# Linear attention and gated FFN on one core: the last residual added whole, and the last pair's end in float32 halves

## The chip, the cores and the metric

The kernel runs on one core of one Trainium2 chip. The metric is the device time of one execution in microseconds (us). A core has a matrix engine (TensorE, PE in the profile; its weight loads are PEld), three element-wise engines (VectorE or DVE, ScalarE or ACT, GpSimd or POOL) and a queue engine (SyncE, SP). Each engine works through its own queue in order; they wait for each other through semaphores. TensorE writes to PSUM, which has eight banks of 128 x 512 float32; SBUF holds everything else.

## The reference

```python
x = L0_attn_inputs_embeds                         # (16, 256, 128)
x = _layernorm(x + _L0_attn_ref(x, Wqkv, bqkv, Wproj, bproj))
x = _layernorm(x + _L0_ffn_ref(x, w_gate, w_up, w_down))

def _L0_attn_ref(x, ...):                         # 12 layers, 16 heads of 8
    for i in range(12):
        q, k, v = split(x @ Wqkv[i].T + bqkv[i])
        att = q @ k.T / sqrt(8)                   # per head, no softmax
        x = (att @ v) @ Wproj[i].T + bproj[i] + x
    return x

def _L0_ffn_ref(x, w_gate, w_up, w_down):         # int weights times 1/127
    h = silu(x @ w_gate.T / 127) * (x @ w_up.T / 127)     # 384 hidden
    return h @ w_down.T / 127
```

The change is in the last line of the main part: the FFN, the residual sum and the second layer norm.

## The kernel before

The attention has no softmax, so the kernel carries a 128 x 130 matrix per batch through the 12 layers instead of the 256 tokens; tokens come back only at the end. This part fills about the first 240 us.

The 16 batches form eight **pairs** (`NP` = 8) of 512 tokens. `ffn(p, prio)` (L578) issues one pair's end. Tokens stand as four chunks of 128. In order:

- **Residual and first norm.** Transposes of the carried matrix (L644), small bf16 pieces of its offset column (L657), then the tokens' products into one bank (L663, L665). `norm` (L590) takes statistics on VectorE (L602, two chunks an instruction), variance (L603), and on GpSimd the power -1/2 (L609); the scaling into `x1` is either one VectorE op (L616) or four ScalarE ops (L621).
- **Transposes of x1** into a bank (`tr_x`, L671). The bank is split into a high part `xh` in float32r, a rounded float32 that TensorE takes in one pass (a copy, L204 on ScalarE), and a low part `xl` (VectorE, L674). Two float32r passes, one of `xh` and one of `xl`, make up one product.
- **Three hidden blocks** of 128 (`NH` = 3). Each has a gate and an up product (L681 and L682, two passes of 512 columns each), SiLU on ScalarE (L684), the multiply on VectorE (L685) into `sg`, a split of `sg` into `hh` (the helper `copy`, L204 on ScalarE or L206 on VectorE) and `hl` (the helper `sub`, L209 on GpSimd or VectorE), and the down product of both (L693, L694), summed over the blocks in one bank.
- **The residual.** The sum after the FFN needs xh + xl. `xh` is added on VectorE (L696) when the bank is read, times 1/127. `xl` comes in by one more TensorE pass in block 0: `id127r`, 127 times the identity, times `xl` (L692).
- **Second norm.** Transposes back to token order (`tr_o`, L702), statistics, variance, negated mean (L605), power and product on GpSimd (L609, L611), four scalings on ScalarE (L625), and a store (L708) from SyncE. For the last pair the transposes go to two banks, VectorE scales the first half (L623) and ScalarE the second, and ScalarE issues that half's store.

`xt`, `qgv`, `kv`, `yhl`, `thl` in the profile are buffers of the attention part that the FFN uses again: `x1` is `kv`, `sg0` is `xt`, `sg1` is in `qgv`, `xh` is `yhl`, `xl` is `thl`.

**What sets the order.** Nothing is issued when it is called. `plan.op(costs, emit, reads, writes, prio)` records an operation with a cost per engine that could do it; `Plan.run` then goes through the ready operations in a modelled time, takes among those that can start earliest the one of lowest `prio` (less a small share of the work behind it), picks its engine and its bank, and emits it. The order of each engine's queue, the choice between ScalarE, VectorE and GpSimd, and the banks all follow from these costs. `prio` rises by `FSTEP` = 0.15 from pair to pair, so eight pairs are interleaved, the earlier ones ahead:

```python
for p in range(NP):
    ffn(p, L + FOFF + FSTEP * p)
```

Of the kernel before, what the change touches and what calls it, by code (L numbers as in the profile page):

```python
# [9 lines left out]
F32 = mybir.dt.float32  # L10
F32R = mybir.dt.float32r
# [3 lines left out]
ALU = mybir.AluOpType  # L15
# [3 lines left out]
L = 12  # L19
B = 16  # L20
T = 256
C = 128
H = 16
D = C // H
NH = 3
PB = 2
NP = B // PB
W = C + 2
QSCALE = 1.0 / 127.0
# [5 lines left out]
N = PB * T  # L35
K = N // 128
# [12 lines left out]
FOFF = -1  # L49
FSTEP = 0.15  # L50
LSTEP = 0.05
WLEAD = 0.6
TAILW = 0.0001
SPARE = 500


# [16 lines left out]
PE, ACT, DVE, POOL, SP = "pe", "act", "dve", "pool", "sp"  # L73
# [19 lines left out]
class Plan:  # L93
# [3 lines left out]
    def op(self, costs, emit, reads=(), writes=(), prio=0.0):  # L97

        o = Op(len(self.ops), costs, emit, prio)
        for v in reads:  # L100
            o.deps.update(v.writers)
        for v in writes:
            o.deps.update(v.writers, v.readers)
            v.writers, v.readers = [o], []
        for v in reads:
            if v not in writes:
                v.readers.append(o)
        o.vals = list(dict.fromkeys([*reads, *writes]))
        for v in o.vals:
            if v.kind:  # L110
                v.left += 1
                v.ops.append(o)
        for d in o.deps:
            d.users.append(o)
        self.ops.append(o)
# [50 lines left out]
def mm32(n=C):  # L166
    return max(220, 4 * n / 2.4 + 8)


def mmr(n):  # L170
    return max(111, 0.447 * n + 5)


def act(n, sbuf=False, pointers=0):
    return (94 if sbuf else 51) + 93 * pointers + n / 1.2


def dve(n, fast=False):
    return 69 + n / (1.92 if fast else 0.96)


def pool(n):
    return 147 + 2.1 * n
# [7 lines left out]
def linear_attention_ffn_kernel(ctx: ExitStack, tc: tile.TileContext, x, xt, wall, wq0, bias, wg, wu, wd, out):  # L191
    nc = tc.nc
# [3 lines left out]
    new = lambda name, shape, dt=F32: sb.tile([128, *shape], dt, name=name)  # L196
# [3 lines left out]
    bank = lambda v: banks[v.slot]  # L200

    def copy(e, dst, src):
        if e == ACT:
            nc.scalar.copy(dst, src)  # L204
        else:
            (nc.vector if e == DVE else nc.gpsimd).tensor_copy(dst, src)  # L206

    def sub(e, dst, a, b):
        (nc.vector if e == DVE else nc.gpsimd).tensor_tensor(dst, a, b, ALU.subtract)  # L209
# [17 lines left out]
    ident = new("ident", [128])  # L227
# [5 lines left out]
    center, centerr = new("center", [128]), new("centerr", [128], F32R)  # L233
    nc.gpsimd.tensor_scalar(center, ident, 1.0, -1.0 / C, ALU.mult, ALU.add)
    nc.vector.tensor_copy(centerr, center)

    id127, id127r = new("id127", [128]), new("id127r", [128], F32R)
    nc.gpsimd.tensor_scalar(id127, ident, 1.0 / QSCALE, 0.0, ALU.mult, ALU.add)
    nc.vector.tensor_copy(id127r, id127)
    mhalf = new("mhalf", [K])  # L240
    nc.gpsimd.memset(mhalf, -0.5)

# [335 lines left out]
    def ffn(p, prio):  # L578
# [8 lines left out]
        def op(costs, emit, reads, writes):  # L587
            plan.op(costs, emit, reads, writes, prio)

        def norm(src, centred, other=None):  # L590


            xs, rows = t("x1"), lambda: bank(src)
            cut = lambda a, k: a[:, k * C : (k + 1) * C]
            row = lambda k: cut(bank(other if other and k >= K // 2 else src), k)

            def stats(e):

                for k in range(0, K, 2):
                    b = bank(other if other and k else src)  # L600
                    both = b[:, k * C : (k + 2) * C].rearrange("p (k c) -> p c k", c=C)
                    nc.vector.bn_stats(t("st")[:, k : k + 2, :].rearrange("p k s -> p (k s)"), both)  # L602
                nc.vector.tensor_scalar(t("ve"), t("st")[:, :, 2], 1.0 / C, EPS, ALU.mult, ALU.add)  # L603
                if not centred:
                    nc.vector.tensor_scalar(t("nm"), t("st")[:, :, 1], -1.0, None, ALU.mult)  # L605
            op({DVE: K // 2 * (dve(2 * C) + 40) + 75 * (2 - centred)}, stats, [src, *([other] if other else [])], [v["st"]])

            def rstd(e):
                nc.gpsimd.tensor_tensor(t("rs"), t("ve"), mhalf, ALU.pow)  # L609
                if not centred:  # L610
                    nc.gpsimd.tensor_tensor(t("nb"), t("nm"), t("rs"), ALU.mult)  # L611
            op({POOL: 1060 + 220 * (not centred)}, rstd, [v["st"]], [v["rs"]])

            def scale(e, ks=range(K)):
                if centred and e == DVE:
                    nc.vector.tensor_tensor(chunks(xs), chunks(rows()), t("rs").unsqueeze(2).to_broadcast([128, K, C]), ALU.mult)  # L616
                    return
                for k in ks:
                    d, r, rs = cut(xs, k), row(k), t("rs")[:, k : k + 1]
                    if centred:  # L620
                        nc.scalar.activation(d, r, AF.Copy, scale=rs)  # L621
                    elif e == DVE:
                        nc.vector.tensor_scalar(d, r, t("st")[:, k, 1:2], rs, ALU.subtract, ALU.mult)  # L623
                    else:
                        nc.scalar.activation(d, r, AF.Identity, bias=t("nb")[:, k : k + 1], scale=rs)  # L625
            if centred:
                costs = {DVE: dve(N), ACT: K * act(C, False, 1)}
            else:
                costs = {ACT: K * act(C, False, 2)}
            if not other:  # L630
                op(costs, scale, [src, v["rs"], v["st"]], [v["x1"]])
                return [v["x1"]]

            ends = [Val(), Val()]
            op({DVE: 2 * 319}, lambda e: scale(e, range(2)), [src, v["rs"], v["st"], v["x1"]], [ends[0]])
            op({ACT: 2 * act(C, False, 2)}, lambda e: scale(e, range(2, K)), [other, v["rs"], v["st"], v["x1"]], [ends[1]])
            return ends


        ptt, pc, pr, px, pd, po = (Val("bank") for _ in range(6))  # L640

        def tr_t(e):
            for b in range(PB):
# [28 lines left out]
        op({PE: K * 109}, tr_x, [v["x1"]], [px])  # L672
        op({ACT: act(N), DVE: dve(N)}, lambda e: copy(e, t("xh"), bank(px)), [px], [v["xh"]])
        op({DVE: dve(N)}, lambda e: nc.vector.tensor_tensor(t("xl"), bank(px), t("xh").bitcast(F32), ALU.subtract), [px, v["xh"]], [v["xl"]])  # L674
        for n in range(NH):
            sg, hh, hlo = f"sg{n % 2}", f"hh{n % NB}", f"hl{n % NB}"
            pgate, pup = Val("bank"), Val("bank")
            for key, o in (("g", pgate), ("u", pup)):
                def mm_x(e, key=key, o=o, n=n):
                    ws = fw[key][:, n * C : (n + 1) * C]  # L680
                    nc.tensor.matmul(bank(o), ws, t("xh"), start=True, stop=False)  # L681
                    nc.tensor.matmul(bank(o), ws, t("xl"), start=False, stop=True)  # L682
                op({PE: 2 * mmr(N)}, mm_x, [v["xh"], v["xl"], vfw[key]], [o])
            op({ACT: act(N)}, lambda e, sg=sg, o=pgate: nc.scalar.activation(t(sg), bank(o), AF.Silu, scale=QSCALE), [pgate], [v[sg]])  # L684
            op({DVE: dve(N)}, lambda e, sg=sg, o=pup: nc.vector.scalar_tensor_tensor(t(sg), bank(o), QSCALE, t(sg), ALU.mult, ALU.mult), [pup], [v[sg]])  # L685
            op({ACT: act(N, True), DVE: dve(N, True)}, lambda e, sg=sg, hh=hh: copy(e, t(hh), t(sg)), [v[sg]], [v[hh]])
            op({POOL: pool(N), DVE: dve(N)}, lambda e, sg=sg, hh=hh, hlo=hlo: sub(e, t(hlo), t(sg), t(hh).bitcast(F32)), [v[sg], v[hh]], [v[hlo]])

            def mm_d(e, n=n, hh=hh, hlo=hlo):
                ws = fw["d"][:, n * C : (n + 1) * C]  # L690
                if n == 0:
                    nc.tensor.matmul(bank(pd), id127r, t("xl"), start=True, stop=False)  # L692
                nc.tensor.matmul(bank(pd), ws, t(hh), start=False, stop=False)  # L693
                nc.tensor.matmul(bank(pd), ws, t(hlo), start=False, stop=(n == NH - 1))  # L694
            op({PE: (2 + (n == 0)) * mmr(N)}, mm_d, [v[hh], v[hlo], v["xl"], vfw["d"]], [pd])
        op({DVE: dve(N)}, lambda e: nc.vector.scalar_tensor_tensor(t("sg0"), bank(pd), QSCALE, t("xh").bitcast(F32), ALU.mult, ALU.add), [pd, v["xh"]], [v["sg0"]])  # L696

        po2 = Val("bank") if p == NP - 1 else None

        def tr_o(e):  # L700
            for k in range(K):
                nc.tensor.transpose(bank(po2 if po2 and k >= K // 2 else po)[:, k * C : (k + 1) * C], t("sg0")[:, k * 128 : (k + 1) * 128], ident)  # L702
        op({PE: K * 109}, tr_o, [v["sg0"]], [po, *([po2] if po2 else [])])
        ends = norm(po, False, po2)
        m = N // len(ends)
        for i, end in enumerate(ends):
# [20 lines left out]
            center_tokens(l, l + 2)  # L727
    prep_ffn(L - 2)
    for p in range(NP):
        ffn(p, L + FOFF + FSTEP * p)  # L730
    plan.run()


# [29 lines left out]
```

## Time and profile before

| | |
|---|---|
| runs shown | 309.02 us median of 3 (308.63 to 309.62) |
| profiled execution | 309.26 us, its span 307.2 us |
| granted TensorE clock, mean | 0.989 |
| busy share of the span: PE, DVE, ACT, POOL | 97%, 74%, 72%, 44% |
| chain that ended last, by engine | PE 88%, DVE 7%, ACT 3% |

The span runs from the first to the last instruction; the execution's time has some 2 us more around it. The groups of instructions that belong to the change, from 240 us on:

| group | count | mean of one |
|---|---|---|
| L692 PE, 127 times the identity, 512 columns | 8 | 448 ns |
| L693, L694 PE, down product, 512 columns | 24, 24 | 402, 404 ns |
| L204 ACT, cast to `hh` | 21 | about 645 ns |
| L206 DVE, cast to `hh` | 3 | 1449 ns (one), 622 ns (two) |
| L209 POOL, `hl` | 14 | 1.30 us |
| L209 DVE, `hl` | 10 | 809 ns (nine), 683 ns (one) |
| L621 ACT, scaling of the first norm, 128 columns | 24 | 399 ns |
| L616 DVE, the same, 512 columns at once | 2 | 682 ns |
| L696 DVE, last sum, 512 columns | 8 | 681 ns |
| L702 PE, transposes back | 32 | 293 ns |

The mean of one is how long its record lasts. Records overlap in an engine's pipeline (a pass of 0.39 us may start 0.23 us after the one ahead), so a sum over a queue is made with the distance between starts.

### The profile page before, as it was taken

The page shows a single profiled execution, that of the slowest core. Times are in us where ns is not written, and L with a number is a line of the kernel's source. Part 1 is how long each engine was busy: PE and PEld are TensorE (multiplying, and loading weights), DVE is VectorE, ACT ScalarE, POOL GpSimd, SP SyncE. Part 2 cuts the span into 40 slices and gives each one's busy share as a digit, 9 for nine tenths or more (in the row PEclk, how much of TensorE's full clock was granted, in tenths as well). Part 3 has the DMA queues.
Part 4 walks back from the last instruction along what each step waited for, and adds up shares of the span by engine and source line. Part 5 has one row for each costly group of instructions (what it writes and reads, how often), then busy time and mean ns, then how long its engine had stood idle before and what let it go on. Part 6 is the DMA issues. An engine that isn't in the chain of part 4 may idle for free.

```text
span 307.2 us, 12904 instructions
## 1 busy us (share of the span) xinstructions
PE 297.3 (97%) x5384; PEld 272.3 (89%) x5384; DVE 227.2 (74%) x680; ACT 221.3 (72%) x571; POOL 136.4 (44%) x234
## 2 busy tenths in 40 slices
PE   8999999999999999999999999999999999999971
PEld 8989999999999999999999999999999988888840
DVE  3797887777677676776767877787554699899993
ACT  2547877867768677777677666776986768968964
POOL 6246353334541345314453144521442456568582
PEclk9999999999999999999999999999999999999995
DMA  7534213122031120311202112130000000000214
GB/s 211 149 99 128 71 39 89 35 55 71 9 82 38 42 84 2 90 37 43 82 4 53 38 28 55 30 81 2 4 2 3 2 1 2 0 0 22 83 34 137
DMA packets 22489, 15.65 MB, mean 51 GB/s; under 512 B 1952, under 2 KB 19872, under 8 KB 22432
## 3 DMA queue, kind: packets, MB, share of 16 engines
q1 hardware_dynamic: 21872, 14.62, 17.5%
q8 instruction: 42, 0.69, 0.9%
q10 hardware_dynamic: 560, 0.22, 0.3%
q14 instruction: 15, 0.12, 0.1%
HBM read 8.02 MB, written 2.10 MB: 33 GB/s over the span
## 4 chain that ended last, share of the span: by engine, by line
PE 88%; DVE 7%; ACT 3%; issue 1%; POOLq 0%; POOL 0%
PE bank L460 14%; PE bank L439 8%; PE bank L522 8%; PE bank L441 7%; PE bank L440 7%; PE bank L447 5%; PE bank L504 5%; PE bank L541 4%; PE bank L539 4%; PE bank L540 4%; PE bank L448 3%; PE bank L449 3%; PE bank L341 3%; PE bank L665 2%; PE bank L681 2%; PE bank L682 2%
## 5 line engine op out<-in xcount | busy, mean ns | idle before, releaser
L209 POOL TENSOR_TENSOR thl<-tst,thl 128x260 fp32r<-128x260 f32 x88 | 64.5, 764 | 122.9 <-ACT thl L204 122.9
L204 ACT COPY qgv<-bank 128x256 f32<-128x256 f32 x171 | 60.8, 376 | 20.5 <-PE bank L449 13.5
L204 ACT COPY kv<-bank 128x512 f32<-128x512 f32 (+1 forms) x93 | 53.3, 575 | 18.6 <-PE bank L441 13.4
L439 PE MATMUL bank<-whl,thl 128*128 128x256 f32 x176 | 51.8, 294 | 0.0
L441 PE MATMUL bank<-whl,thl 128*128 128x256 f32 x176 | 49.6, 282 | 0.0
L440 PE MATMUL bank<-whl,thl 128*128 128x256 f32 x176 | 49.4, 281 | 0.0
L460 PE MATMUL bank<-kv,g 128*128 128x128 f32 x352 | 46.0, 275 | 0.0
L546 DVE TENSOR_TENSOR tst<-bank,tst 128x260 f32<-128x260 f32 x96 | 36.9, 425 | 11.9 <-PE bank L541 9.1
L204 ACT CAST thl<-tst 128x260 fp32r<-128x260 f32 x88 | 33.0, 408 | 14.6 <-DVE tst L546 14.5
L460 PEld LDWEIGHTS bank<-kv,g 128*128 128x128 f32 x352 | 42.7, 191 | 0.4 <-issue 0.4
L453 DVE TENSOR_SCALAR qgv<-bank,bcol 128x2 f32<-128x2 f32 x88 | 19.3, 221 | 27.6 <-ACT qgv L204 23.0
L439 PEld LDWEIGHTS bank<-whl,thl 128*128 128x128 f32 x176 | 33.1, 188 | 4.1 <-issue 4.0
L535 DVE TENSOR_TENSOR yhl<-bank,yhl 128x260 fp32r<-128x260 f32 x96 | 34.3, 421 | 2.4 <-ACT yhl L204 2.4
L440 PEld LDWEIGHTS bank<-whl,thl 128*128 128x128 f32 x176 | 33.2, 189 | 0.0
L441 PEld LDWEIGHTS bank<-whl,thl 128*128 128x128 f32 x176 | 33.1, 188 | 0.0
L447 PE MATMUL bank<-thl,whl 128*128 128x260 f32 x88 | 29.0, 329 | 0.0
L522 PE MATMUL bank<-qgv,gm 32*32 32x130 f32 x1536 | 25.9, 280 | 0.2 <-DVE gm L212 0.2
L204 ACT CAST yhl<-bank 128x260 fp32r<-128x260 f32 (+1 forms) x61 | 22.3, 418 | 5.2 <-PE bank L522 3.8
L206 DVE CAST yhl<-bank 128x260 fp32r<-128x260 f32 x43 | 16.5, 424 | 11.8 <-PE bank L522 11.8
L448 PE MATMUL bank<-thl,whl 128*128 128x260 f32 x88 | 24.8, 282 | 0.0
L449 PE MATMUL bank<-thl,whl 128*128 128x260 f32 x88 | 24.7, 281 | 0.0
L522 PEld LDWEIGHTS bank<-qgv,gm 32*32 32x32 f32 x1536 | 17.3, 103 | 5.6 <-ACT kv L204 0.3
(153 smaller groups left out, 705.8 us busy)
## 6 DMA issues: line engine op xcount, KB each, us to landing
wraw<-wall SPq DMA_DIRECT2D x12, 256.0 KB, 3.0
wpt<-whl SPq DMA_DIRECT2D x24, 96.0 KB, 2.2
qgv<-x SPq DMA_DIRECT2D x8, 256.0 KB, 5.4
xt<-xt SPq DMA_DIRECT2D x8, 256.0 KB, 3.3
out<-kv SPq DMA_DIRECT2D x7, 256.0 KB, 2.3
wpt<-whl SPq DMA_DIRECT2D x24, 64.0 KB, 2.6
wpt<-whl SPq DMA_DIRECT2D x24, 32.0 KB, 1.9
wraw<-wg SPq DMA_DIRECT2D x1, 192.0 KB, 3.4
```

Of the source, the lines that this page charges most:

```text
L204: nc.scalar.copy(dst, src)
L209: (nc.vector if e == DVE else nc.gpsimd).tensor_tensor(dst, a, b, ALU.subtract)
L439: nc.tensor.matmul(o, hi[:, b, 0:C], hl(0, 1, 2), start=True, stop=False)
L440: nc.tensor.matmul(o, hi[:, b, 0:C], hl(1, 1, 2), start=False, stop=False)
L441: nc.tensor.matmul(o, lo[:, b, 0:C], hl(0, 1, 2), start=False, stop=True)
L447: nc.tensor.matmul(o, hl(0, 0), flat(hi), start=True, stop=False)
L448: nc.tensor.matmul(o, hl(0, 0), flat(lo), start=False, stop=False)
L449: nc.tensor.matmul(o, hl(1, 0), flat(hi), start=False, stop=True)
L460: nc.tensor.matmul(bank(pgv)[:, b * C : (b + 1) * C], g0[p][:, b, :], tv(b), start=True, stop=True)
L522: nc.tensor.matmul(bank(pys[r])[group(g + r), b * W : (b + 1) * W], gm[group(g), r * PB + b, :], qss[p][group(g), b, :], start=True, stop= ...
L535: plan.op({DVE: dve(PB * W)}, lambda e: nc.vector.tensor_tensor(yl, bank(py)[:, : PB * W], yh.bitcast(F32), ALU.subtract), [py, vyh[p]], [ ...
L546: plan.op({DVE: dve(PB * W)}, lambda e: nc.vector.tensor_tensor(ts, bank(pw)[:, : PB * W], ts, ALU.add), [pw], [vt[p], vc[p]], prio)
```

## The change

- `id127`, `id127r` and the pass L692 are removed. `xl` no longer enters the bank of the down products.
- After the split into `xh` and `xl`, a new operation `whole` writes x1 in transposed order over `x1`: ScalarE copies it from the transposes' bank, or GpSimd adds `xh` and `xl`; the planner chooses. The last sum adds this instead of `xh`.
- For the last pair only (p = 7): the down products go to two banks, 256 columns each. In its third block `sg` isn't split; two plain float32 products (`mm_direct`) take it whole. The last sum, the transposes and the statistics are recorded for each half by itself, and the sum is written to `sg1`'s buffer.
- `norm`'s statistics and its variance become separate operations where there are two banks.
- The last pair's `prio` is lowered by `AHEAD` = 0.16, a little more than one step.

```diff
+AHEAD = 0.16
...
-    id127, id127r = new("id127", [128]), new("id127r", [128], F32R)
-    nc.gpsimd.tensor_scalar(id127, ident, 1.0 / QSCALE, 0.0, ALU.mult, ALU.add)
-    nc.vector.tensor_copy(id127r, id127)
...
+            if other:
+                parts = [Val(), Val()]
+                for k, b in ((0, src), (2, other)):
+                    op({DVE: some}, lambda e, k=k: stats(e, [k]), [b], [parts[k // 2]])
+                op({DVE: tiny}, var, parts, [v["st"]])
+            else:
+                op({DVE: K // 2 * some + tiny}, lambda e: (stats(e), var(e)), [src], [v["st"]])
...
+        def whole(e):
+            if e == ACT:
+                nc.scalar.copy(t("x1"), bank(px))
+            else:
+                nc.gpsimd.tensor_tensor(t("x1"), t("xh").bitcast(F32), t("xl").bitcast(F32), ALU.add)
+        op({ACT: act(N), POOL: pool(N)}, whole, [px, v["xh"], v["xl"]], [v["x1"]])
+
+        cut = 2 if p == NP - 1 else 1
+        downs = [(Val("bank"), slice(i * N // cut, (i + 1) * N // cut)) for i in range(cut)]
+        outs, total = [Val("bank") for _ in range(cut)], "sg1" if cut == 2 else "sg0"
...
-            op({ACT: act(N, True), DVE: dve(N, True)}, lambda e, sg=sg, hh=hh: copy(e, t(hh), t(sg)), [v[sg]], [v[hh]])
-            op({POOL: pool(N), DVE: dve(N)}, lambda e, sg=sg, hh=hh, hlo=hlo: sub(e, t(hlo), t(sg), t(hh).bitcast(F32)), [v[sg], v[hh]], [v[hlo]])
-
-            def mm_d(e, n=n, hh=hh, hlo=hlo):
-                ws = fw["d"][:, n * C : (n + 1) * C]
-                if n == 0:
-                    nc.tensor.matmul(bank(pd), id127r, t("xl"), start=True, stop=False)
-                nc.tensor.matmul(bank(pd), ws, t(hh), start=False, stop=False)
-                nc.tensor.matmul(bank(pd), ws, t(hlo), start=False, stop=(n == NH - 1))
-            op({PE: (2 + (n == 0)) * mmr(N)}, mm_d, [v[hh], v[hlo], v["xl"], vfw["d"]], [pd])
-        op({DVE: dve(N)}, lambda e: nc.vector.scalar_tensor_tensor(t("sg0"), bank(pd), QSCALE, t("xh").bitcast(F32), ALU.mult, ALU.add), [pd, v["xh"]], [v["sg0"]])
...
+            direct = n == NH - 1 and p == NP - 1
+            if not direct:
+                op({ACT: act(N, True), DVE: dve(N, True)}, lambda e, sg=sg, hh=hh: copy(e, t(hh), t(sg)), [v[sg]], [v[hh]])
+                op({POOL: pool(N), DVE: dve(N)}, lambda e, sg=sg, hh=hh, hlo=hlo: sub(e, t(hlo), t(sg), t(hh).bitcast(F32)), [v[sg], v[hh]], [v[hlo]])
+            ws = fw["d"][:, n * C : (n + 1) * C]
+            for i, (d, cols) in enumerate(downs):
+                def mm_d(e, n=n, ws=ws, sg=sg, hh=hh, hlo=hlo, d=d, cols=cols):
+                    o = bank(d)[:, cols]
+                    nc.tensor.matmul(o, ws, t(hh)[:, cols], start=(n == 0), stop=False)
+                    nc.tensor.matmul(o, ws, t(hlo)[:, cols], start=False, stop=(n == NH - 1))
+
+                def mm_direct(e, n=n, ws=ws, sg=sg, d=d, cols=cols):
+                    nc.tensor.matmul(bank(d)[:, cols], ws.bitcast(F32), t(sg)[:, cols], start=False, stop=(n == NH - 1))
+                m = N // len(downs)
+                if direct:
+                    op({PE: mm32(m)}, mm_direct, [v[sg], vfw["d"]], [d])
+                else:
+                    op({PE: 2 * mmr(m)}, mm_d, [v[hh], v[hlo], vfw["d"]], [d])
+        sums = [Val() for _ in downs]
+        for (d, cols), o, r in zip(downs, outs, sums):
+            m = N // len(downs)
+            op({DVE: dve(m)}, lambda e, d=d, cols=cols: nc.vector.scalar_tensor_tensor(t(total)[:, cols], bank(d)[:, cols], QSCALE, t("x1")[:, cols], ALU.mult, ALU.add), [d, v["x1"]], [r])
+
+            def tr_o(e, o=o, cols=cols):
+                for k in range(cols.start // 128, cols.stop // 128):
+                    nc.tensor.transpose(bank(o)[:, k * C : (k + 1) * C], t(total)[:, k * 128 : (k + 1) * 128], ident)
+            op({PE: m // 128 * 109}, tr_o, [r], [o])
+        po, po2 = outs if len(outs) == 2 else (*outs, None)
...
-    ffn(p, L + FOFF + FSTEP * p)
+    ffn(p, L + FOFF + FSTEP * p - (AHEAD if p == NP - 1 else 0))
```

The rest follows from the planner. In the new order of instructions the first 240 us are as before but for the two set-up operations. Behind them, `whole` runs on ScalarE for six pairs and on GpSimd for pairs 1 and 3; the first norm's scaling is on VectorE for five pairs (before: two) and on ScalarE for three (before: six); of the 23 splits left, `hh` is cast on ScalarE 19 times and on VectorE 4 times, and `hl` is subtracted on GpSimd 15 times and on VectorE 8 times.

More of the change, by code (lines that the diff above doesn't have):

```diff
@@ L595, in norm, with stats @@
             row = lambda k: cut(bank(other if other and k >= K // 2 else src), k)
-            def stats(e):
-                for k in range(0, K, 2):
+            def stats(e, ks=range(0, K, 2)):
+                for k in ks:
                     b = bank(other if other and k else src)
@@ L602, in stats, with var @@
                     nc.vector.bn_stats(t("st")[:, k : k + 2, :].rearrange("p k s -> p (k s)"), both)
+            def var(e):
                 nc.vector.tensor_scalar(t("ve"), t("st")[:, :, 2], 1.0 / C, EPS, ALU.mult, ALU.add)
@@ L605, in stats @@
                     nc.vector.tensor_scalar(t("nm"), t("st")[:, :, 1], -1.0, None, ALU.mult)
-            op({DVE: K // 2 * (dve(2 * C) + 40) + 75 * (2 - centred)}, stats, [src, *([other] if other else [])], [v["st"]])
+            some, tiny = dve(2 * C) + 40, 75 * (2 - centred)
+            if other:
[5 more added lines that the diff above has]
+                op({DVE: K // 2 * some + tiny}, lambda e: (stats(e), var(e)), [src], [v["st"]])
             def rstd(e):
@@ L637, in norm @@
             return ends
-        ptt, pc, pr, px, pd, po = (Val("bank") for _ in range(6))
+        ptt, pc, pr, px = (Val("bank") for _ in range(4))
         def tr_t(e):
@@ L695, in ffn @@
-            op({PE: (2 + (n == 0)) * mmr(N)}, mm_d, [v[hh], v[hlo], v["xl"], vfw["d"]], [pd])
[L696 to L702, printed above, removed]
@@ L703, in ffn @@
-        op({PE: K * 109}, tr_o, [v["sg0"]], [po, *([po2] if po2 else [])])
+            direct = n == NH - 1 and p == NP - 1
[15 more added lines that the diff above has]
+                    op({PE: 2 * mmr(m)}, mm_d, [v[hh], v[hlo], vfw["d"]], [d])
```

## The prediction

> Pairs are counted 0 to 7 and hidden blocks 0 to 2, so up(6,2) is the up product of pair 6, block 2. Times are us from the start of the profiled span.
>
> **What bounds it now.** I read the page's slices first, then the busy time by stretches, then the timeline of single instructions.
>
> ```profile
> PE   8999999999999999999999999999999999999971
> DVE  3797887777677676776767877787554699899993
> ...
> 284.00:294.00 10.00, 10.00 (x51) 8.24 (x50) 9.28 (x20) 7.85 (x18) 6.67 (x7) 1.00 0.24 68
> 294.00:299.00 5.00, 3.13 (x17) 1.81 (x14) 4.80 (x16) 3.73 (x10) 4.22 (x7) 1.00 0.16 43
> 299.49:302.11 2.62, 1.12 (x4) 0.71 (x4) 1.79 (x5) 2.51 (x8) 0.63 (x3) 0.63 0.58 160
> ```
>
> In the stretches the columns are stretch, length, busy PE, PEld, DVE, ACT, POOL, granted clock, DMA share, GB/s. TensorE is full to the 38th slice, and VectorE is nearly full from 274 on. Busy TensorE proves little, so the starts of its instructions decide:
>
> ```profile
> 292.93 0.39 PE L694 MATMUL bank<-hl,wfd 128*128 128x512 f32 x1
> 293.16 0.39 PE L681 MATMUL bank<-yhl,wfu 128*128 128x512 f32 x1
> 293.39 0.39 PE L682 MATMUL bank<-thl,wfu 128*128 128x512 f32 x1
> ...
> 294.99 0.40 PE L694 MATMUL bank<-hl,wfd 128*128 128x512 f32 x1
> 296.57 0.63 PE L702 MATMUL bank<-ident,xt 128*128 128x128 f32 x4 [1.19 <-DVE xt L696]
> ```
>
> Passes start 0.23 apart and start almost without gaps from about 255 to 294.99. The two at 293.16 are up(7,2), the last gate/up product. It ends at 293.62; I call that end U. Up to U the stage is TensorE's. After it comes a tail of latencies. The chain that ended last, in order of time:
>
> ```profile
> 298.31 0.60 DVE hl L209
> 298.92 0.04 issue
> 298.96 0.51 PE bank L694
> 299.47 0.02 issue
> 299.49 0.70 DVE xt L696
> 300.19 0.04 issue
> 300.24 0.70 PE bank L702 x2
> 300.94 0.02 issue
> 300.96 0.87 DVE st L602 x2
> ```
>
> Low half, down pass, sum, transposes and statistics follow one another, each waiting for the one before.
>
> **The change, part by part.**
>
> (1) *Identity pass removed.* Eight passes of L692 go. Their record is 448 ns, but what counts is the distance of starts: 276.14, 276.37, 276.61 in the timeline, 0.233. Seven of the eight stand ahead of U (the last, pair 7's, follows at 294.43): 7 x 0.233 = **-1.63**, as long as TensorE stays the one that waits for nobody. The 256-wide halves of pair 7's down products are neutral: 8 passes of about 0.12 (the 260-wide L448 starts 0.12 apart) for 4 of 0.233, and they come after U. The set-up of the identity (one small op on POOL, one on DVE) is hidden behind the first loads, which land after 5.4.
>
> (2) *Whole residual added.* Eight copies or additions, 512 wide: six on ACT (row: 575 ns for a 512-wide PSUM copy), two on POOL (row: 1.30 for a 512-wide tensor-tensor). ACT gives back 12 of its 24 scale pieces of L621 (1.15 for 4 at 251 to 265, some 0.29 each) and two casts (0.65): 6 x 0.575 - 12 x 0.29 - 2 x 0.65 = -1.3 on ACT, which was 78% busy. DVE takes three more 512-wide scales (0.60 from start to start) and a cast (0.42), loses two low halves (0.60) and trades some small copies: +3 x 0.60 + 0.42 - 2 x 0.60 + 0.1 = +1.1. I cost this at nothing, because before 274 DVE has room: idle 1.1 in 250 to 260, 0.9 in 260 to 268 and 0.3 in 268 to 274. Without that cover it costs its 1.1. The copy is also a third reader of the transposed bank, so the bank comes free one ACT copy later: between 0 and 0.6 if a product waits there. By the new order at least ten products (4.7) lie between the transposes and the bank's next use, against 0.63 + 0.68 + 0.58 for its three readers, so I take 0.
>
> (3) *The tail, up to the last sum.* In the new order pair 7 runs level with pair 6. From the end of up(6,2) to the new U, TensorE has ten products of two passes and two groups of four transposes (0.44): 10 x 0.466 + 0.88 = 5.54. VectorE, from its multiply of (6,2) to the first half of the last sum, has nine 512-wide ops and four groups of statistics (0.93: 297.38 to 298.31 in the chain): 9 x 0.60 + 4 x 0.93 = 9.12. It starts 0.27 after up(6,2) ends (a lone pass shows 0.50 against 0.23 of distance), if VectorE isn't late then; being late by all of its +1.1 is rival B. So the last sum starts at U + 0.27 + 9.12 - 5.54 = U + 3.85; today it is at 299.49 = U + 5.87: **-2.02**. What makes this possible is the missing cast, subtraction and wait of (7,2). The plain float32 product that replaces them has no row at 256 columns. L665's float32 passes take 0.111 per 128 columns, two to a product (eight in 0.89), so a half should take 0.44; the fp32r row (0.12) and twice 0.44 at half clock bound it. It hides behind pair 6's statistics: 0.08 + 0.05 + 0.44 + 0.27 = 0.84 against 0.93. At half clock it would put up to 0.8 on the path. The multiply needs the last SiLU, which now stands on ACT behind the final scaling of pair 3 (1.37 for four), which waits for POOL's power (1.0) and product. By the same durations that SiLU ends some 1.2 before VectorE wants it.
>
> (4) *Last sum by halves.* Sum of 256 columns (record 0.42, as 256-wide copies), transposes 0.72 to the statistics (300.24 to 300.96), the second half 0.35 behind: 0.35 + 0.42 + 0.05 + 0.72 + 0.43 for its statistics + 0.28 for L603 and L605 = 2.25 against 299.49 to 302.11 = 2.62: **-0.37**. Splitting the statistics op adds no instruction. Behind 302.11 nothing changes: POOL power, half on DVE, half on ACT, two stores. SP still issues the seven stores of 256 KB in order and then the first half of pair 7; pair 6's scaling on ACT still ends before pair 7's.
>
> (5) *Stalls.* VectorE and POOL get in each other's way:
>
> ```profile
> 274.64 1.29 POOL L209 TENSOR_TENSOR hl<-qgv,hh 128x512 fp32r<-128x512 f32 x1 [1.94 <-ACT hh L204]
> 274.77 1.45 DVE L206 CAST hh<-xt 128x512 fp32r<-128x512 f32 x1
> ...
> 291.25 1.30 POOL L209 TENSOR_TENSOR hl<-xt,hh 128x512 fp32r<-128x512 f32 x1
> 291.32 1.78 DVE L209 TENSOR_TENSOR hl<-xt,hh 128x512 fp32r<-128x512 f32 x1
> ```
>
> The cast takes 0.42 elsewhere and the subtraction 0.68, so these cost 1.03 and 1.10, and both end just after POOL does. POOL's long ops grow from 14 to 17, and VectorE's ops of this kind shrink from 13 to 12. My step (3) has none in it; I allow one, **+1.06**, with 0 and 3 x 1.06 as bounds.
> The Trainium skill (SBUF — State Buffer, section "SBUF: two separate sides") calls the port pair of the two engines an exclusive lock for the whole instruction, for a VectorE op with two SBUF inputs too; these rows agree, and by it every overlap costs up to a POOL op. That speaks against giving POOL two more such ops; rival C is that case.
>
> Sum: -1.63 - 2.02 - 0.37 + 1.06 = **-2.96**. The profiled span of 307.2 becomes 304.2. That execution took 309.26, 2.06 more than its span and 0.24 above the median of the runs shown; against the median 309.02 the forecast is **306.0**.
>
> On the clock: it is 1.00 until 299.49 and 0.63 on average in the 2.62 behind, so it halves near 300.2, five after TensorE's dense stretch ended. If the shorter tail keeps it whole, the last transposes take 0.35 less (0.60 instead of 1.12 for four); I leave that in the range.
> The Trainium skill (TensorE: Matmul & The Clock Gate, "What's actually happening") has the clock halve after an idle window of about 3.4 us; by it the new tail, under four long, would mostly run whole, about 305.7.
>
> **Rivals.**
> A, *no stall and a whole clock*: -4.02 - 0.35, **304.6**. For it: fewer VectorE ops that can collide. Against it: two collisions in the last 35 us now.
> B, *VectorE is the bound*: the passes taken from TensorE are worth nothing, VectorE's +1.1 counts, the idle 0.59 ahead of the last sum goes, the halves save 0.37: +0.1, **309.2**. For it: VectorE busy 9.28 of 10 in 284 to 294. Against it: today it begins the multiply of (6,2) at 288.94, 0.32 after TensorE allows it (288.35 + 0.27), so the two are level and neither alone sets the pace.
> C, *VectorE the bound and locked out by POOL*: B with one to three further waits for a 512-wide POOL op, 1.06 each: **310.2** to 312.4. Place: VectorE's low halves and casts of pairs 3 to 7 against POOL's 17 long ops. It decides from the first stall on, given B. For it: the rows in (5). Against it: in the new order both ops on VectorE's side become fewer.
> D, *the bank doesn't come free*: TensorE waits for ACT's whole copies and loses what it saved: -2.02 - 0.37 + 1.06, **307.7**. For it: ACT feeds nearly every bank. Against it: 4.7 of room for 1.9 of reading.
>
> **Chances and range.** Forecast 0.45, A 0.16, D 0.14, B 0.11, C 0.14. A measurement of this kernel tells about 0.3% (0.93) from no change. Faster: forecast, A and D, 0.75; within: B, 0.11; slower: C, 0.14. The range 304.3 to 309.8 leaves out the lower part of A and nearly all of C. The forecast's own range is 304.9 (no stall) to 307.2 (two stalls).
>
> **What would show it.** No identity rows; down passes still 0.23 apart up to the last up product, which then ends near 292.0; the last sum 3 to 5 after it, two 256-wide ops back to back behind pair 6's statistics; float32 passes of 0.22 each, two per half; the power of pair 7 near 299. Wrong would be: gaps on TensorE before 290 released by ACT's copies (D), VectorE ops above 1 us beside POOL ones (C), or the last SiLU waiting behind pair 3's scaling.

## The result, and the profile after

The changed kernel takes 306.49 us (median of 6 runs, 305.67 to 307.59) against 309.32 for the kernel before beside it: a ratio of 0.9914, with a 95% interval of 0.9886 to 0.9941. Its profiled execution spans 304.6 us instead of 307.2. The lines PE, DVE and PEclk (the granted clock) are from its slices; the others are its stretches, with the columns of the stretches of before.

```profile
PE   8999999999999999999999999999999999989981
DVE  4796877777677676876768777786545689999993
...
PEclk9999999999999999999999999999999999999998
...
260.00:268.00 8.00, 7.23 (x40) 5.73 (x38) 7.86 (x14) 5.88 (x13) 4.84 (x5) 1.00 0.00 0
284.00:294.00 10.00, 10.00 (x52) 8.20 (x51) 9.90 (x23) 8.98 (x22) 8.79 (x10) 1.00 0.19 53
297.34:299.41 2.07, 1.04 (x6) 0.40 (x4) 1.80 (x8) 2.04 (x6) 1.21 (x3) 1.00 0.46 131
```

The kernel before, in the same stretch:

```profile
260.00:268.00 8.00, 8.00 (x43) 6.54 (x42) 7.11 (x15) 7.79 (x20) 3.60 (x4) 1.00 0.00 0
```

TensorE, full from 260 to 268 before, has lost 0.77 there. VectorE is full from 284 to 294 (9.90 instead of 9.28). The stretch from the last sum to the last power is 2.07 instead of 2.62 long, at a clock of 1.00 instead of 0.63. The timeline of single instructions has the new end:

```profile
292.98 0.40 PE L701 MATMUL bank<-thl,wfu 128*128 128x512 f32 x1
...
296.54 1.13 PE L717 MATMUL bank<-xt,wfd 128*128 128x256 f32 x4 [0.82 <-DVE xt L704]
297.34 0.79 DVE L726 SCALAR_TENSOR_TENSOR qgv<-bank,kv 128x256 f32<-128x256 f32 x2
297.92 0.71 PE L730 MATMUL bank<-ident,qgv 128*128 128x128 f32 x4 [0.25 <-DVE qgv L726]
298.36 0.76 DVE L599 BATCH_NORM_STATS2 st<-bank 128x6 f32<-128x256 f32 x2 [0.23 <-PE bank L730]
299.41 1.01 POOL L615 TENSOR_TENSOR rs<-ve,mhalf 128x4 f32<-128x4 f32 x1 [0.69 <-DVE nm L604]
```

The last up product ends at 292.98 + 0.23 = 293.21, the last sum (its two halves back to back) starts at 297.34, the power at 299.41. In the chain of waits the stretch from 291.55 to the last sum is now VectorE's; this is its end:

```profile
294.36 0.59 DVE xt L726
294.95 0.68 DVE st L599 x2
295.63 0.02 issue
295.65 0.17 DVE ve L602
295.82 0.07 DVE nm L604
295.89 0.59 DVE xt L704
296.48 0.68 DVE st L599 x2
297.16 0.02 issue
297.19 0.11 DVE ve L602
297.30 0.04 issue
297.34 0.44 DVE qgv L726
```

Sum of pair 6, statistics of pair 5, multiply of (7,2), statistics of pair 6 and last sum follow each other with no wait for another engine. The float32 passes are not in the chain. The timeline of VectorE goes further back: its last wait for another engine is this one.

```profile
274.64 0.69 DVE L210 TENSOR_TENSOR hl<-xt,hh 128x512 fp32r<-128x512 f32 x1 [0.46 <-ACT hh L205]
```

From there to the last sum, 22.7 us, VectorE never stands idle for more than 0.06 at a time.

**Where the time went.** The way into the loops varies between executions: one projection pass of the eleventh layer (the 196th of the 216 that read `wpt`), ahead of all that the kernels here do differently, starts between 223.42 and 225.14 in their traces. So I count from that pass, the mark. One profiled execution each, us from the mark; U is the end of the last up product:

| kernel | median | ratio to before, 95% | U | last sum | power | end |
|---|---|---|---|---|---|---|
| before | 309.32 | | 69.46 | 75.33 | 77.95 | 83.0 |
| changed | 306.49 | 0.9914 (0.9886 to 0.9941) | 69.22 | 73.35 | 75.42 | 80.6 |
| changed, again (control) | 306.04 | 0.9904 (0.9878 to 0.9930) | 69.20 | 73.28 | 75.34 | 80.5 |
| no identity pass | 308.42 | 0.9973 (0.9957 to 0.9990) | 67.80 | 74.74 | 77.35 | 82.4 |
| no whole copies | 306.15 | 0.9896 (0.9877 to 0.9915) | 68.76 | 72.84 | 74.90 | 80.1 |
| two ops moved | 305.87 | 0.9891 (0.9875 to 0.9908) | 68.33 | 72.68 | 74.74 | 79.9 |
| AHEAD 0 | 309.59 | 1.0018 (1.0005 to 1.0031) | 71.08 | 76.38 | 78.48 | 83.7 |
| last block split | 308.34 | 0.9978 (0.9960 to 0.9995) | 69.23 | 74.92 | 77.17 | 82.3 |
| one sum | 307.84 | 0.9957 (0.9941 to 0.9973) | 69.16 | 73.71 | 76.05 | 81.9 |
| float32 (7,0) | 306.62 | 0.9914 (0.9890 to 0.9938) | 69.22 | 73.04 | 75.10 | 81.1 |
| moved, float32 (7,0), (6,2) | 305.65 | 0.9878 (0.9857 to 0.9898) | 68.33 | 72.56 | 74.61 | 79.8 |
| moved, and (7,1) | 306.07 | 0.9901 (0.9883 to 0.9919) | 68.33 | 72.95 | 75.00 | 80.2 |
| before, level | 308.63 | 0.9976 (0.9958 to 0.9993) | 68.01 | 73.71 | 76.58 | 82.4 |
| moved, float32 (7,0) | 306.09 | 0.9904 (0.9874 to 0.9934) | 68.32 | 72.14 | 74.19 | 80.1 |

The changed kernel's U differs by 0.02 between its two traces, and by 0.07 over the five rows that share its order up to there, so shifts of 0.1 can be read up to U. In the two rows that are planned anew (AHEAD 0, and before, level) U is another point of the work, as one down product more or two fewer stand ahead of it; their last sums can be compared with the others, their U cannot. By this count the change brings -0.24 up to U, -1.74 from U to the last sum, -0.55 from there to the power and +0.1 behind it. With -0.17 ahead of the mark that makes -2.6, the difference of the spans.

### The profile page after: what moved, and what is told of

Read it like the earlier page. It is cut to its first block, busy times and chain, and to the rows that moved or that the text cites. A ratio compares the mean times of both kernels' runs of the same rounds, so it can differ in the third digit from the quotient of the medians.

```text
span 304.6 us, 12894 instructions
## 1 busy us (share of the span) xinstructions
PE 295.0 (97%) x5382; PEld 270.8 (89%) x5382; DVE 226.6 (74%) x685; ACT 221.2 (73%) x564; POOL 140.7 (46%) x232
## 4 chain that ended last, share of the span: by engine, by line
PE 81%; DVE 11%; ACT 3%; issue 3%; POOL 0%; POOLq 0%; DVEq 0%
PE bank L457 14%; PE bank L436 8%; PE bank L519 8%; PE bank L438 7%; PE bank L437 7%; PE bank L501 5%; PE bank L444 5%; PE bank L538 4%; PE bank L537 4%; PE bank L536 4%; PE bank L445 3%; PE bank L446 3%; PE bank L338 3%; DVE st L599 2%; DVE xt L704 2%
```

## Experiments: the passes taken away

**No identity pass.** The kernel before, its order kept, with the pass left out:

```diff
-                if n == 0:
-                    nc.tensor.matmul(bank(pd), id127r, t("xl"), start=True, stop=False)
-                nc.tensor.matmul(bank(pd), ws, t(hh), start=False, stop=False)
+                nc.tensor.matmul(bank(pd), ws, t(hh), start=(n == 0), stop=False)
```

> The kernel before with the eight identity passes left out and every queue otherwise in the same order (the low part of x1 is missing from the last sum). If TensorE sets the pace up to the last up product, that product ends up to 1.6 us earlier and the time falls by 0.9 to 1.6. If VectorE sets the pace, the time stays within 0.4 of the kernel before.

U comes 1.66 earlier, seven passes of 0.237. The last sum comes only 0.59 earlier, and the median is 0.8 below that of the kernel before beside it, a little less than the 0.9 to 1.6 expected. Where the other 1.07 goes stands in its timeline and in one of its stretches (the last line):

```profile
295.21 0.93 PE L700 MATMUL bank<-ident,xt 128*128 128x128 f32 x4 [1.63 <-DVE xt L694]
...
296.18 0.76 DVE L602 BATCH_NORM_STATS2 st<-bank 128x6 f32<-128x256 f32 x2 [0.17 <-PE bank L700]
...
297.13 0.68 DVE L209 TENSOR_TENSOR hl<-xt,hh 128x512 fp32r<-128x512 f32 x1
297.86 0.80 PE L692 MATMUL bank<-hl,wfd 128*128 128x512 f32 x1 [0.44 <-DVE hl L209]
298.70 0.69 DVE L694 SCALAR_TENSOR_TENSOR xt<-bank,yhl 128x512 f32<-128x512 f32 x1 [0.89 <-PE bank L692]
...
296.00:297.00 1.00, 1.00 (x4) 0.56 (x3) 0.79 (x4) 1.00 (x3) 0.98 (x1) 0.50 0.10 30
```

About half of it is VectorE. Its last wait ahead of these lines ends at 285.77, by the mark 1.16 earlier than in the kernel before (287.13), not 1.66, and from there it works without a wait. The other half is TensorE's clock. It is 0.50 from 296 on (0.85 on average from 294 to 296), where the kernel before has 1.00 up to 300. The transposes take 0.93 instead of 0.63, so that the statistics behind them come 0.90 earlier, and the last pass takes 0.80 instead of 0.50, which leaves 0.59. So the saving on TensorE is real, and most of it is lost in this order, to a VectorE that has no room left and to a clock that halves nearly five us sooner.

**No whole copies.** In the changed kernel `whole` emits nothing, and the last sum adds what its buffer holds.

```diff
-        op({ACT: act(N), POOL: pool(N)}, whole, [px, v["xh"], v["xl"]], [v["x1"]])
+        op({ACT: act(N), POOL: pool(N)}, lambda e: None, [px, v["xh"], v["xl"]], [v["x1"]])
```

> The changed kernel with the eight whole copies left out, order of the rest unchanged (the last sum adds what stands in the buffer instead of x1). If the copies are hidden, as the prediction costed them, the time stays within 0.4 of the changed kernel. Rival: the two GpSimd additions and the longer hold of the banks cause the gap of 1.2 us on TensorE at 267; then that gap goes and the time falls by about 1.2.

U is 0.46 earlier, the last sum 0.51; the median is 0.34 below that of the changed kernel beside before, and 0.11 above the one taken again. That is within the 0.4 expected, and the copies cost between nothing and 0.5. The half us at U is one wait at 267 that shrinks from 1.02 to 0.53, the wait of the next run.

**Two operations moved.** What TensorE waits for at 267 in the changed kernel, from its timeline:

```profile
264.58 1.58 POOL L210 TENSOR_TENSOR hl<-xt,hh 128x512 fp32r<-128x512 f32 x1 [1.65 <-ACT hh L205]
...
265.04 1.67 DVE L210 TENSOR_TENSOR hl<-qgv,hh 128x512 fp32r<-128x512 f32 x1
...
266.64 0.75 DVE L599 BATCH_NORM_STATS2 st<-bank 128x6 f32<-128x256 f32 x2
...
267.50 1.29 DVE L704 SCALAR_TENSOR_TENSOR xt<-bank,xt 128x512 f32<-128x512 f32 x2
...
268.25 0.50 PE L713 MATMUL bank<-hh,wfd 128*128 128x512 f32 x1 [1.02 <-DVE xt L704]
```

VectorE's subtraction for (1,1) takes 1.67 instead of 0.68, beside GpSimd's; pair 7's first statistics and the multiply of (3,0) behind it are late by as much, and the next down product waits 1.02 for that multiply to clear its bank. The experiment keeps the order but for the cast and subtraction of (1,1), which go behind that multiply:

```diff
+MOVES = [([('hi', 1, 1), ('lo', 1, 1)], ('mul', 3, 0))]
...
+        for names, behind in MOVES:
+            some = [self.tags[n] for n in names]
+            order = [o for o in order if o not in some]
+            at = order.index(self.tags[behind]) + 1
+            order[at:at] = some
```

> The changed kernel with VectorE's cast and subtraction of pair 1, block 1 (the subtraction that took 1.67 us beside GpSimd's) moved behind pair 7's statistics and the multiply of pair 3, block 0. If that one lock-out made the gap of 1.2 us on TensorE at 267, the gap goes, the last up product ends about 1.2 earlier and the time falls by 0.8 to 1.2. If the gap had another cause, it stays and the time is within 0.3.

The wait is gone. U comes 0.89 earlier and the last sum 0.67, so the stall is the larger part of the 1.42 by which the changed kernel's U is behind that of the kernel with no identity pass. The 0.67 is what VectorE gains: its run without a wait starts at 50.64 from the mark in the changed kernel and at 49.98 here. The median is 0.62 and 0.17 below the two of the changed kernel, less than the 0.8 to 1.2 expected, and the intervals of the ratios overlap, so a shorter time isn't shown. What is left of the 1.42, 0.53, stands in the weight loads of this trace:

```profile
244.97 0.42 PEld L688 LDWEIGHTS bank<-ident,kv 128*128 128x128 f32 x4 [0.36 <-ACT qgv L216]
...
271.90 0.19 PEld L711 LDWEIGHTS bank<-yhl,wfg 128*128 128x128 f32 x1 [0.40 <-ACT kv L696]
```

Transposes that wait for a ScalarE copy start 0.29 late at 244.98 (0.40 behind the one ahead instead of 0.11), and so they do in the changed kernel at 244.08. The gate product at 271.90 waits for a whole copy (`kv` is `x1`), and its two passes take 0.23 more than two starts at the usual distance. Another 0.12 goes at 270.27, to a multiply. These three make 0.64 against the 0.53, so no large loss is left unplaced.

## Experiments: the tail

**AHEAD 0, planned anew.** The last pair's priority no longer lowered (`AHEAD = 0.0`).

> The changed kernel with AHEAD = 0, so that the last pair comes behind pair 6 again; all of the FFN part is planned anew. If running level is what shortens the tail, the distance from the last up product to the last sum grows by 0.5 to 1.5 and so does the time. Rival: the float32 product and the halves do it alone; then the time is within 0.4.

All that the change brings is gone: 309.59, with the last sum 3.03 later than in the changed kernel. From U to the sum it is 1.17 more, as expected; the time grows by 3.1, twice the most that was expected. U is 1.86 later too, 0.9 of it for a down product and four transposes more that stand ahead of it. The last sum waits 0.86 for the float32 product here. A product also waits for a whole copy, for 0.34:

```profile
265.73 0.50 PE L700 MATMUL bank<-yhl,wfg 128*128 128x512 f32 x1 [0.34 <-ACT kv L685]
```

**The last pair level in the kernel before.** Only the priority, planned anew:

```diff
-        ffn(p, L + FOFF + FSTEP * p)
+        ffn(p, L + FOFF + FSTEP * p - (AHEAD if p == NP - 1 else 0))
```

> The kernel before with nothing but the last pair's priority lowered by 0.16, planned anew; the identity passes, the split of the last block and the whole sum stay. Theory (level order pays only where the last block has no cast and subtraction behind pair 6's statistics; the split alone cost the changed kernel 2.3, and the identity passes stay): 308.6 to 310. Rival (the order alone makes the shorter tail): 307.0 to 308.0.

The last sum comes 1.62 earlier though block (7,2) is split as ever: the planner puts its subtraction ahead of pair 6's sum, at 296.70. The median gains only 0.24% (0.8 us), as the level order makes pair 7's statistics and power queue behind pair 6's (2.87 instead of 2.62 from sum to power) and the stores end later. The time, 308.63, is just inside the range of my theory; the theory itself, that level order pays only without the split, is wrong as far as the last sum goes.

**The last block split.** The changed kernel without its float32 product. The order is kept, but the final scaling of pair 5 on ScalarE goes behind the new cast:

```diff
-    nc.tensor.matmul(bank(d)[:, cols], ws.bitcast(F32), t(sg)[:, cols], start=False, stop=(n == NH - 1))
+    if cols.start == 0:
+        copy(ACT, t(hh), t(place))
+        sub(DVE, t(hlo), t(place), t(hh).bitcast(F32))
+    nc.tensor.matmul(bank(d)[:, cols], ws, t(hh)[:, cols], start=False, stop=False)
+    nc.tensor.matmul(bank(d)[:, cols], ws, t(hlo)[:, cols], start=False, stop=(n == NH - 1))
```

(`place` is the buffer that holds `sg`.)

> The changed kernel, order kept, but block 2 of pair 7 is split again: cast on ScalarE, subtraction on VectorE behind pair 6's statistics, two float32r passes for each half; the halves and the level order stay. Theory (the plain float32 product takes the subtraction and its wait off the path): from the start of the subtraction to the start of the sum took 1.18 before (298.31 to 299.49), so the first half of the sum comes 1.0 to 1.2 later than in the changed kernel, 307.5 to 307.7. Rival (the level order alone made the shorter tail, the float32 product is worth nothing): 306.2 to 306.8.

```profile
298.55 0.69 DVE L224 TENSOR_TENSOR hl<-xt,hh 128x512 fp32r<-128x512 f32 x1 [0.29 <-ACT hh L219]
...
299.30 0.39 PE L747 MATMUL bank<-hl,wfd 128*128 128x256 f32 x1 [0.34 <-DVE hl L224]
...
299.79 0.76 DVE L757 SCALAR_TENSOR_TENSOR qgv<-bank,kv 128x256 f32<-128x256 f32 x2 [0.55 <-PE bank L747]
```

At the same U the sum starts 1.57 to 1.64 later than in the two traces of the changed kernel. 0.29 of it is a wait for the cast, which I had left behind a scaling of pair 4 on ScalarE, so about 1.3 is the subtraction and its wait, against 1.0 to 1.2 expected; the last transposes then run in part at half clock (the granted clock is 0.73 from 300 to 301), with 2.25 from sum to power against 2.07. The time, 308.34, is above the expected range too. In this order the float32 product is needed; the run before shows that in another order the last sum comes early without it.

**One sum, 512 wide.** Pair 7's products and sum in one bank, order kept:

```diff
+    if len(downs) == 2:
+        if cols.start:
+            return
+        d, cols = downs[0][0], slice(0, N)
...
+        def both(e):
+            one = bank(downs[0][0])
+            nc.vector.scalar_tensor_tensor(t(total), one, QSCALE, t("x1"), ALU.mult, ALU.add)
```

> The changed kernel, order kept, but pair 7's down products, its plain float32 product and the last sum are 512 columns wide, in one bank and one instruction each. Theory: the sum waits for the whole product, 0.08 + 0.05 + 0.88 + 0.27 = 1.28 behind the last multiply instead of 0.93, so +0.35, and the chain from the sum to its statistics is longer by 0.1 to 0.4: 306.9 to 307.2. Rival (the halves are worth nothing, as the second half ends where one whole would): 306.3 to 306.6.

```profile
296.89 1.12 PE L749 MATMUL bank<-xt,wfd 128*128 128x512 f32 x2 [0.82 <-DVE xt L722]
...
298.12 0.69 DVE L758 SCALAR_TENSOR_TENSOR qgv<-bank,kv 128x512 f32<-128x512 f32 x1 [0.34 <-PE bank L749]
...
298.96 0.63 PE L765 MATMUL bank<-ident,qgv 128*128 128x128 f32 x4 [0.95 <-DVE qgv L758]
```

The sum waits 0.34 for the whole product, where the half hid behind pair 6's statistics, and sum to power takes 2.34 at whole clock instead of 2.06: 0.71 in all to the power. The median, 307.84, is above the expected range and 1.8 above the control beside it; 0.7 of the rest goes behind the power (see the last section), and 0.4 I can't place.

**The changed kernel again,** beside these three:

> The changed kernel as it is, beside the three others: 306.5, with 306.2 to 306.8 as what the same kernel may show again.

306.04. The twelve runs of both comparisons have a median of 306.30.

## Experiments: which engine sets the last nine us

The down product of a block in float32 takes a cast and a subtraction away and makes TensorE's passes longer (0.88 for 512 columns). All keep the changed kernel's order. First only (7,0), whose subtraction VectorE had; (7,2) then uses a buffer of pair 0:

```diff
+DIRECT = {(7, 0), (7, 2)}
+SKIPPED = {(k, p, n) for p, n in DIRECT for k in ("hi", "lo")}
...
+    if (p, n) in DIRECT:
+        nc.tensor.matmul(bank(d)[:, cols], ws.bitcast(F32), t(place)[:, cols], start=(n == 0), stop=(n == NH - 1))
+        return
```

> The changed kernel, order kept, but block 0 of pair 7 also goes down in plain float32, without its cast (ScalarE) and its subtraction (VectorE, 0.60); block 2 then uses pair 0's buffer. Theory (from the multiply of pair 6, block 2 to the last sum VectorE has no gap, so its work sets the end): the last sum comes 0.6 earlier, 305.9. Rival (TensorE sets the end there; its passes for this product grow from four of 0.12 to 0.88): 306.5 to 306.9.

The last sum comes 0.24 earlier than in the control, not 0.60, and the median, 306.62, is in the rival's range: VectorE now waits for an up product.

```profile
290.98 0.69 DVE L722 SCALAR_TENSOR_TENSOR qgv<-bank,qgv 128x512 f32<-128x512 f32 x1 [0.23 <-PE bank L716]
```

Then, with the two operations moved, more blocks: (6,2) as well, then (7,1) too, then (7,0) alone.

> The changed kernel, order kept, with the cast and subtraction of pair 1, block 1 moved behind pair 7's first statistics and pair 3's first multiply (as in the earlier run with those two moved, 305.87), and with pair 7's block 0 and pair 6's block 2 going down in plain float32 too, so that VectorE has two subtractions (0.60 each) less in the last nine us and ScalarE two casts. Theory (VectorE sets the end from the multiply of pair 6, block 2, once TensorE is not late): the last sum comes 0.6 to 1.2 earlier than with the move alone, 304.7 to 305.3. Rival (TensorE sets the end there too; the two products grow by 0.42 each): 305.9 to 306.5.

> As the run beside it, and pair 7's block 1 in plain float32 as well: ScalarE loses one more cast and GpSimd one 1.29 subtraction in the last six us; TensorE gets 0.42 more behind the last up product. Theory (VectorE sets the end): 0 to 0.3 below the run beside it. Rival (TensorE or the last SiLU sets the end): 0.1 to 0.4 above it.

> The changed kernel, order kept, with the cast and subtraction of pair 1, block 1 moved as before (that move alone gave 305.87, its last sum 4.35 behind the last up product), and pair 7's block 0 in plain float32, so without its cast and its subtraction (0.60 on VectorE); pair 6's block 2 and pair 7's block 1 stay split. Alone, the float32 block 0 brought the last sum forward by 0.24 only, as VectorE then waited 0.23 for an up product; here TensorE is 0.9 further on. Theory (VectorE sets the end once TensorE is not late): the last sum 0.5 to 0.6 earlier than with the move alone, some 3.8 behind the last up product, 305.2 to 305.4. Rival (TensorE's longer products or a lock-out by GpSimd take up what VectorE saves, as in the two runs with more float32 products): 305.7 to 306.1.

Against the move alone the last sum comes 0.12 earlier with (6,2), 0.27 later with (7,1) too, and 0.54 earlier with (7,0) alone. Where the subtractions' 1.2 went in the first of the three:

```profile
292.05 1.28 POOL L224 TENSOR_TENSOR hl<-qgv,hh 128x512 fp32r<-128x512 f32 x1
...
292.62 0.74 DVE L616 TENSOR_SCALAR ve<-st 128x4 f32<-128x4 f32 x1
...
293.71 0.69 DVE L750 SCALAR_TENSOR_TENSOR xt<-bank,kv 128x512 f32<-128x512 f32 x1 [0.28 <-PE bank L734]
```

and in the second:

```profile
293.30 0.69 DVE L750 SCALAR_TENSOR_TENSOR xt<-bank,kv 128x512 f32<-128x512 f32 x1 [0.85 <-PE bank L734]
...
295.90 0.76 DVE L613 BATCH_NORM_STATS2 st<-bank 128x6 f32<-128x256 f32 x2 [0.38 <-PE bank L754]
```

A lock-out and waits for the longer float32 passes take back what VectorE saves. With (6,2) the time, 305.65, lies between the theory's and the rival's; with (7,1) too it is 0.42 above the run beside it, as by the rival. With (7,0) alone neither happens, and 0.54 of 0.60 arrives at the sum: there VectorE does set the last sum, as long as TensorE isn't late. The gain is not in the median (306.09 against 305.87, in the rival's range): 0.7 goes behind the power, where the stores end later. The lowest median, 305.65, is 0.65 under the pooled changed kernel, but the intervals of the ratios overlap; no run settles whether it is faster.

## Why the prediction was right, step by step

The forecast was 306.0 and -2.96; measured are 306.49 and, in the spans, -2.6.

1. *Identity passes, -1.63.* Right as a price: -1.66 alone. In the changed kernel only -0.24 of it is left at U, which the forecast had near 292.0 and which is at 293.21. By the starts of its passes TensorE loses 1.28 in the stall at 267 and 0.29 at 244.08. The condition "as long as TensorE stays the one that waits for nobody" is what failed.
2. *Whole residual, 0.* Right within the bounds: 0 to 0.5. Its cover held but for what it adds to the stall at 267. The wait for the bank that rival D needs doesn't show in the changed kernel; it shows in other orders, with 0.34 at AHEAD 0 and 0.23 with the two operations moved.
3. *Tail, -2.02.* The lengths are right, the size is -1.74: the sum starts at U + 4.13, not 3.85. TensorE's part was 5.52 (forecast 5.54, from the end of up(6,2) at 287.69 to U); VectorE's part ran without a gap from 288.02 to 297.34, 9.32 (forecast 9.12), and its start was 0.33 behind up(6,2), not 0.27. 0.17 of the 0.20 is one variance op beside a GpSimd subtraction, 0.34 instead of 0.17. The float32 half was hidden as worked out: the sum starts right behind pair 6's statistics. What the forecast had wrong is that the sum hangs on U. VectorE had not waited for anyone since 274.64 and was 0.06 behind TensorE at up(6,2), level with it by chance; with the two operations moved U comes 0.89 earlier and the sum 0.67. That the missing split is what makes the short tail possible was too strong: level order alone moves the sum by 1.62, and at AHEAD 0 it goes with all else.
4. *Sum by halves, -0.37.* It became -0.55: the clock stayed whole, which I had left in the range (with 0.35 more, so -0.72 by my figures). By the Trainium skill (TensorE: Matmul & The Clock Gate, "What's actually happening") the clock halves after an idle window of about 3.4 us. The trace of the changed kernel agrees: TensorE's last instruction ends at 298.63, and the mean clock is 1.00 to 302 and 0.54 from 302 to 303. Two other traces don't, if idle means without any instruction. In the kernel before the clock halves near 300.2, with a pass from 298.96 to 299.46; with no identity pass it halves near 295.4, behind a gap of only 1.63 (293.58 to 295.21). So how much work keeps the clock whole stays open.
5. *One stall, +1.06.* The size was right (1.02), the place not: I looked at pairs 3 to 7, but it fell on pair 1 at 265 and reached TensorE, so that it took from step 1 and not from step 3. VectorE ops above 1 us beside GpSimd's, my sign of rival C, did show (1.67 at 265.04, 1.02 at 255.35). A cast at 279.98, 1.00 instead of 0.43, lies in VectorE's run without a wait; what it costs was not tried.

Behind the power, forecast as unchanged, there is +0.1.

The nearness of the sum is partly luck. Up to U, passes and stall together were -0.57 in the forecast and are -0.24; the tail falls short by 0.28; the halves give 0.18 more, and the way into the loops, which the change doesn't touch, 0.17. (The bound with two stalls adds up to 307.1, not 307.2.)

Rival A lost by the stall, though its whole clock came. B is half right: VectorE sets the 22.7 us up to the last sum, but it was not late against TensorE there, and the tail became shorter all the same. Of C the lock-out came, once with effect on TensorE. D needs waits for the whole copies, and the changed kernel has none; the ScalarE copy that TensorE waits for at 244.08 is another.

## What to carry to other kernels

A saving on the engine that is full reaches the end only if what stands behind it can follow: alone, the passes brought 1.66 at the last product and 0.59 at the last sum, as VectorE was level with TensorE and the clock of the last passes halved sooner. A full TensorE and a last product don't tell which engine sets the end; look for the last wait of each engine. Where two engines are level, taking an op from one is worth its time only up to the slack of the other (0.54 of 0.60 where TensorE was ahead, 0.24 where it was not). Look for lock-outs between VectorE and GpSimd in the whole stage, not only near the end, and move the one op whose lateness another engine waits for.

## What was not expected of the hardware

Not only 512-wide ops on VectorE are stretched beside GpSimd. From the timeline of the changed kernel:

```profile
255.07 1.27 POOL L210 TENSOR_TENSOR hl<-xt,hh 128x512 fp32r<-128x512 f32 x1
255.35 1.02 DVE L602 TENSOR_SCALAR ve<-st 128x4 f32<-128x4 f32 x1
...
270.72 1.62 POOL L210 TENSOR_TENSOR hl<-qgv,hh 128x512 fp32r<-128x512 f32 x1 [0.49 <-ACT hh L205]
...
284.21 0.76 POOL L617 TENSOR_TENSOR nb<-nm,rs 128x4 f32<-128x4 f32 x1
```

A variance of four columns takes 1.02 instead of 0.17, with one SBUF input; and GpSimd loses too (1.62 instead of 1.29, 0.76 instead of 0.20). The Trainium skill (SBUF — State Buffer, "SBUF: two separate sides") has whichever side starts first block the other. The first two pairs of rows bear that out, one in each direction (a VectorE subtraction runs from 270.50). In the last row GpSimd loses though its record starts 0.02 ahead of VectorE's subtraction (284.23), so the order of such close starts isn't to be read from the records.

The time behind the power is 5.1 to 5.2 in ten of the fourteen traces and 5.8 to 6.0 in four: one sum, float32 (7,0) with and without the move, and the level order in the kernel before. In these the two last stores land 2.3 to 3.0 after their issue instead of 1.9. DMA issues of the changed kernel (the first line; its other store is the same) and of the one with the move and (7,0):

```profile
out<-kv SPq DMA_DIRECT2D x1, 128.0 KB, 1.9
```

```profile
out<-kv SPq DMA_DIRECT2D x1, 128.0 KB, 2.7
out<-kv ACTq DMA_DIRECT2D x1, 128.0 KB, 2.6
```

The medians of these four kernels are also worse than their power times say (float32 (7,0): power 0.24 earlier than the control, median 0.58 later), so it seems to belong to the kernel and not to the one execution. Its cause was not found.
